# First loads on one queue in a fixed order, sums of x on VectorE, and a new order table in a seven-product interaction kernel

## The chip, the core and the metric

The kernel runs on one core of a Trainium2 chip. The metric is the device time of one execution in microseconds, as the median of several runs. A core has TensorE (PE; its weight loads are listed apart as PEld), VectorE (DVE), ScalarE (ACT), GpSimd (POOL) and SyncE (SP), and 16 DMA engines that all of them share. Plain transfers are issued here by SP, and a few by ACT; transfers that add what they bring to what lies in the destination are issued by POOL.

## What is computed

```python
out_lin = x @ lin_w.T + lin_b                                      # x: 1024 x 512
xv = jnp.einsum('bf,efm->bem', x, weight)                          # weight: 64 x 512 x 512
zp = jnp.einsum('bf,efm->bem', jnp.square(x), jnp.square(weight))
interaction = 0.5 * jnp.sum(jnp.square(xv) - zp, axis=1)
return out_lin + interaction                                       # 1024 x 512, float32
```

The sum over e of x² against weight² needs weight² only as its sum over e, so this is one matmul of the size of `x @ lin_w.T`. The large part is xv: x against 64 times 512 columns of weight, squared and summed over e.

## The kernel before

All matmuls are float32. Products of two matrices are made with seven products of quarters instead of eight (Strassen's scheme in Winograd's form), which trades matmuls for sums of operands and of results. It is used twice over, and the names follow from it.

**Outer level.** x (transposed, 512 features by 1024 rows) is cut into four quarters `x_in(h, q)`, h a half of the rows, q a half of the features. X1, X2 and X4 are copies of the quarters (0,0), (0,1), (1,1), made on ACT. X5 = x(1,1) - x(1,0), X6 = X5 - x(0,0) with a sign, X7 and X3 are combinations made on VectorE. The weight has four quarters too, w11, w12, w21, w22, and three sums: T1 (of the second and first quarter), T2 = a quarter + T1, then w12 + w22 and w21 + T2. These sums are not calculated by an engine: an adding transfer issued by POOL brings one operand into the other (`outer_sum`, L708 to L717, with `dma_add`, L480). Likewise, the results od are added to ob, and od to oc (`outer_out`, L719).

**Inner level.** Each of the seven pairs (X1 with w11, X6 with T2, X5 with T1, X2 with w21, X7 with w12, X4 with w21 + T2, X3 with w22, in this order, the constant `ORDER`) is multiplied again by seven products (`tree`, L749), or, for four of the seven in groups of 24 columns, by 20 products (`wide_tree`, L838). For this, each X gets further sums of its own four blocks: s1, s2, s4 and a new a21, four sums of 128x256 per X, 28 in all (L656 to L659). They go through `tt` (L438), which gives every sum that reads no PSUM to POOL unless it is told `only=DVE`. `widen` (L661) makes the further blocks for the trees of 20 later. The sums of weight blocks (tile `t`) are on POOL too.

**Stages.** The program begins with a memset and two warm-up matmuls of zeros (L554 to L559). Then `lin` (L623) makes x @ lin_w.T with the seven products of the outer level: 16 PE records each of 256 columns, at L543, in the order x1, x2, x4, x5, x6, x7, x3. It needs the quarters of lin_w, `lw(q, c)`, and sums of these (`lsum`), made on VectorE. Its four results go to DRAM (`lind`) and come back at the end. Then come 22 groups of columns of the weight, two of 16 columns and 20 of 24, each with the seven trees (L490). A group loads six pieces of weight on SP (`load`, L701). The squares of weights (ACT) are summed on VectorE (`w_squares`, L725), and so are the squares of xv (`finish`, L734). At the end the seven outer products of x² against the sums of weight² are made, on the same code as lin, and added to what lin left and to the accumulated sums (`accd`).

**PSUM.** Four pairs of banks, b1, b3, b2_0 and b2_1. A tree starts two products in b3 and two in b1, copies b1 to b2 on ACT, copies b3 to p5 and p53, and adds in the banks; the results leave to oa, ob, oc and od through VectorE. Trees of neighbouring pairs overlap on PE.

**What sets the order.** No order is written by hand. `Plan.add` (L171) takes each operation with its cost on an engine, and `Plan.order` (L196) goes through the program with these costs, giving each engine the most urgent operation that is ready. The urgency is the latest time at which it may start, less an entry of the table `AHEAD_OF` (in eighths of a microsecond, base 36). Every kind of operation in every part of the program has such an entry, so a new table can change the order on every engine. Each engine then runs its instructions strictly in the planned order, and each waits for its operands.

**The first loads.** x comes in eight transfers of 128x512 (0.262 MB) on SP; lw in four of the same size on ACT, through an argument `queue` of `dma` (L477) that only these use; then the bias. All are ordered by the planner.

Of the kernel before, what the change touches and what calls it, by code (L numbers as in the profile page):

```python
# [12 lines left out]
AF = mybir.ActivationFunctionType  # L13
# [28 lines left out]
i:-g j:4x k:t l:-8 m:-2k n:1x o:4i6 p:2c q:9 r:-1w s:n t:-11 u:-1 v:-o w:17 x:1n y:1z z:k 10:-23 11:g 12:-16  # L42
13:4 14:24 15:r 16:-5 17:z 18:j 19:-k 1a:13 1b:-18 1c:e 1d:-2z 1e:4 1f:21 1h:17 1i:-f 1j:-k 1k:-1 1l:1m 1m:-5
1n:-26 1o:-o 1p:q 1q:-b 1r:1p 1s:-22 1t:9 1u:-10 1v:-5 1w:8 1x:-9 1y:i 1z:1u 20:1e 21:-10 22:o 23:-n 24:-2x
25:2 26:-2t 27:-1z 28:2c 29:1b 2a:1z 2b:-b 2c:22 2d:-23 2e:1p 2f:4 2g:-2y 2h:-j 2i:1h 2j:o 2k:9 2l:k 2m:-c
2n:1i 2o:-1z 2p:-2 2q:47 2r:2n 2s:-6 2t:c 2u:-20 2v:10 2w:-2 2x:-m 2y:-10 2z:i 30:4p 31:5c 32:1j 33:9 34:2x
35:n 36:-6 37:-2c 38:d 39:1e 3a:-n 3b:r 3c:1t 3d:j 3e:m 3f:2k 3g:-2s 3h:1v 3i:31 3j:-12 3k:-m 3l:-2f 3m:7b
3n:2 3o:1co 3p:-i 3q:e 3r:-1h 3s:1nz 3t:-1l 3u:3 3v:118 3w:17 3x:-x 3y:-1t 3z:n 40:r 41:4 42:-v 43:18 44:2pm
45:1j 46:-l 47:-t 48:-1c 49:l3 4a:b 4b:2g 4c:e 4d:36 4e:y 4f:1v 4g:16 4h:-q 4i:b 4j:1 4l:-1r 4m:-3c 4n:n 4o:z
4p:-f 4q:-1d 4r:13 4s:5 4t:y 4u:2g 4v:4 4w:1i 4x:1c 4y:-20 4z:1z 50:l 51:-12 52:-20 53:27 54:-z 55:9 56:-2s  # L50
57:1o5 58:g 59:-1j 5a:-2r 5b:2k 5c:i 5d:21 5e:-12 5f:-1q 5g:1ju 5h:2d 5i:25 5j:p 5k:-1l 5l:-k 5m:-1y 5n:3b
5o:h 5p:-3r 5q:20 5r:-28 5s:-b 5t:2a 5u:29 5v:-n 5w:-2b 5x:w1 5y:3 5z:-1e 60:22 61:-1u 62:24i 63:-1u 64:-33
65:5m 66:-r 67:3q 68:-13 69:11 6a:22 6b:p 6c:s 6d:-y 6e:e 6f:25 6g:k 6h:-o 6i:-1n 6j:1c 6k:-u 6l:u 6m:e8
6n:-2f 6o:-1j 6p:z 6q:1m 6r:23 6s:-x 6t:h 6u:-15 6v:-29 6w:-y 6x:15 6y:-6j 6z:19 70:-n 71:-1n 72:-7 73:1u
74:-1n 75:-2c 76:-1e 77:3p 78:1q 79:7 7a:-2 7b:-u 7c:16 7d:-t 7e:-13 7f:-13 7g:-m 7h:u 7i:-1 7j:1c 7k:2b 7l:1p
7n:r 7o:-d 7p:b 7q:-w 7r:-3a 7s:u 7t:-20 7u:-v 7v:2c 7w:-32 7x:-8c 7y:1a 7z:-5 80:2i 81:-e 82:-2a 83:-2j
84:-29 85:-27 86:-j 87:d 88:-16 89:-2v 8a:-1g 8b:-c 8c:fk 8d:-c 8e:-g 8f:-2d 8g:-k 8h:i 8i:1i 8j:z 8k:-5
8l:-1a 8m:-dh 8n:-a 8o:-d1 8p:a 8q:-k 8r:-f 8s:s 8t:28 8u:q 8v:-19 8w:-1b 8x:3n 8y:-26 8z:fo 90:2s 91:-24 92:b
93:a2 94:-6 95:1h 96:1f 97:2q 98:-2u 99:-39 9a:-1j 9b:-m 9c:-2e 9d:28 9e:-s 9f:yw 9g:-l 9h:-16 9i:-w 9j:a
9k:ln 9l:-j 9m:1 9n:n 9o:1s 9p:-17 9q:r 9r:2p 9s:7 9t:-i 9u:m 9v:41 9w:3h 9x:-2c 9y:-s 9z:-17 a0:7 a1:-t a2:j  # L60
a3:-1x a4:1p a5:5 a6:-a a7:2k a8:-2g a9:14 aa:-u ab:-r ac:-14 ad:7 ae:-r af:-1a ag:-1w ah:-d ai:1vp aj:1a
ak:14 al:-1n am:-v an:w ao:-1b ap:1s aq:u ar:z as:11 at:-11 au:1q av:15 aw:j ax:-1b ay:-2i az:1d b0:-38 b1:-3t
b2:-k b3:n b4:-4 b5:-e b6:-j b7:-17 b8:le b9:-x ba:-1a bb:c0 bc:1 bd:he be:3m bf:-x bg:1u3 bh:a bi:38 bj:1sj
bk:-1j bl:c bm:-4q bn:-13 bo:-3h bp:1 bq:-4n br:-1j bs:1de bt:3w bu:1j bv:-8 bw:26 bx:17 by:d bz:-1c c0:-26
c1:3o c2:2c c3:1v c4:t c5:-2h c6:-4 c7:-2g c8:-h0 c9:y ca:3c cb:-u cc:-7i cd:-1 ce:-12 cf:-i cg:c ch:-2j
ci:-92 cj:-m ck:y cl:-1a cm:-m cn:7 co:10 cp:-19 cq:-i cr:-q cs:-15 ct:-1 cu:g cv:10 cw:19p cx:2g cy:-46 cz:2
d0:-1e d1:-1f d2:vf d3:s d4:-r d5:l9 d6:c8 d7:4r d8:-13 d9:-39 da:-t db:rq dc:-w dd:11 de:4o dg:d dh:-3 di:h
dj:-1b dk:2i dl:-b dm:-39 dn:3 do:1 dp:w dq:-1 dr:-r ds:4 dt:-6g du:-4 dv:20 dw:-5o dx:-3o dy:-1r dz:1t e0:3r
e1:-m e2:e e3:1d e4:-1b e5:b e6:-1j e7:-e9 e8:-6 e9:-cq ea:3c eb:1mv ec:-y ed:m ee:w ef:1x eg:1q eh:-1z ei:-w
ej:1l ek:-h el:2 em:f en:30 eo:b ep:1h eq:14 er:o es:6b et:-3 eu:-u ev:10x ew:1f ex:-x ey:-b ez:s f0:-2k f1:m  # L70
f2:-3r f3:e f4:1l f5:p f6:24 f7:-19 f8:9 f9:-4f fa:9ny fb:35 fc:-69 fd:d fe:-1a ff:-1k fg:g fh:z fi:-20 fj:cs
fk:-1i fl:-17f fm:1x fn:-7 fo:2w fp:h fq:jm fr:1s fs:n ft:mz fu:d fv:g fw:fq fx:p fy:-1y fz:-o g0:-h g1:-1x
g2:-4k g3:265 g4:15 g5:-m g6:-g g7:1t g8:-1m g9:-2b ga:-18 gb:2z gc:-9 gd:-2l ge:-1p gf:12 gg:8b gh:1k gi:2bs
# [1089 lines left out]
```

## Time and profile before

| | |
|---|---|
| median of three runs | 1412.26 us (1411.76 to 1416.25) |
| the profiled execution | 1414.87 us, of which span 1413.1 |
| granted TensorE clock, mean | 0.994 |
| busy share of the span | PE 98%, VectorE 83%, POOL 83%, ScalarE 58% |
| PE matmul records | 5500 (two for each float32 matmul) |
| chain that ended last | 91% PE, 4% DMA, 3% POOL |

The times of single steps below come from the one profiled execution. A row of the profile names source line, engine, operation, output tile and input tiles (with buffer numbers left out, so that w11, w12 and w21 all read `w`, T2 reads `T`, and X1 to X7 read `X`). Busy time of PE is no measure of PE at its peak, because matmuls overlap; where it counts, the distance from one matmul to the next is used.

### The profile page before, as it was taken

The page shows a single profiled execution, that of the slowest core. Times are in us where ns is not written, and L with a number is a line of the kernel's source. Part 1 is how long each engine was busy: PE and PEld are TensorE (multiplying, and loading weights), DVE is VectorE, ACT ScalarE, POOL GpSimd, SP SyncE. Part 2 cuts the span into 40 slices and gives each one's busy share as a digit, 9 for nine tenths or more (in the row PEclk, how much of TensorE's full clock was granted, in tenths as well). Part 3 has the DMA queues.
Part 4 walks back from the last instruction along what each step waited for, and adds up shares of the span by engine and source line. Part 5 has one row for each costly group of instructions (what it writes and reads, how often), then busy time and mean ns, then how long its engine had stood idle before and what let it go on. Part 6 is the DMA issues. An engine that isn't in the chain of part 4 may idle for free.

```text
span 1413.1 us, 17921 instructions
## 1 busy us (share of the span) xinstructions
PE 1388.7 (98%) x5500; PEld 1034.9 (73%) x5500; DVE 1179.7 (83%) x1769; ACT 825.7 (58%) x1345; POOL 1173.6 (83%) x1118
## 2 busy tenths in 40 slices
PE   7999999999999999999999999999999999999998
PEld 5878767677776767777776777777677777767666
DVE  5577788888988888888888888888888888898876
ACT  3355555757566565756656565666656565665752
POOL 5999978888788878878887887888788798888884
PEclk8999999999999999999999999999999999999999
DMA  8588595867859596775959577595957759594775
GB/s 248 150 191 195 111 254 126 221 164 178 202 122 243 122 232 154 184 195 127 242 115 247 144 179 199 134 236 116 254 136 183 194 145 228 117 257 117 162 171 131
DMA packets 94943, 251.85 MB, mean 178 GB/s; under 512 B 30464, under 2 KB 33536, under 8 KB 94848
## 3 DMA queue, kind: packets, MB, share of 16 engines
q0 software_dynamic: 27712, 136.23, 49.3%
q1 hardware_dynamic: 66560, 113.43, 23.6%
q10 hardware_dynamic: 576, 1.05, 0.2%
q8 instruction: 45, 0.74, 0.2%
q14 instruction: 50, 0.41, 0.1%
HBM read 127.04 MB, written 6.19 MB: 94 GB/s over the span
## 4 chain that ended last, share of the span: by engine, by line
PE 91%; DMA 4%; POOL 3%; issue 1%; DVE 1%; ACT 0%; SPq 0%; POOLq 0%; ACTq 0%
PE b L490 40%; PE b_r L490 24%; PE b_l L490 24%; POOL t L446 2%; PE b_l L543 2%; PE b_r L543 1%; DMA T<-T1b 1%; DMA oc<-od 1%; DMA T<-T1a 1%; DMA oa<-xT 1%; POOL ob L482 0%; DMA T1a<-weight 0%; DMA w22a<-weight 0%; POOL X L446 0%; DVE oa L446 0%
## 5 line engine op out<-in xcount | busy, mean ns | idle before, releaser
L490 PE MATMUL b<-t,X 128*128 128x384 f32 (+1 forms) x1184 | 401.9, 471 | 3.8 <-DVE ob L446 2.1
L446 POOL TENSOR_TENSOR t<-t,w 128x512 f32<-128x512 f32 (+1 forms) x300 | 293.9, 998 | 36.0 <-PE b L490 25.2
L490 PEld LDWEIGHTS b<-t,X 128*128 128x128 f32 x1184 | 219.2, 190 | 131.2 <-DVE ob L446 10.1
L490 PE MATMUL b_l<-t,X 128*128 128x256 f32 x960 | 243.4, 380 | 0.0
L490 PE MATMUL b_r<-t,X 128*128 128x256 f32 x800 | 214.8, 380 | 0.2 <-POOL t L446 0.2
L490 PEld LDWEIGHTS b_l<-t,X 128*128 128x128 f32 x960 | 180.7, 190 | 34.1 <-ACT b_l L456 2.5
L446 POOL TENSOR_TENSOR t<-w 128x768 f32<-128x768 f32 (+1 forms) x88 | 160.2, 1824 | 33.2 <-DMA w<-T 21.2
L490 PEld LDWEIGHTS b_r<-t,X 128*128 128x128 f32 x800 | 150.3, 190 | 46.0 <-issue 2.8
L463 ACT ACTIVATE oa<-oa 128x768 f32<-128x768 f32 (+1 forms) x176 | 142.7, 823 | 58.6 <-DVE oa L446 47.7
L473 DVE TENSOR_REDUCE acc<-oa 128x12 f32<-128x768 f32 (+1 forms) x176 | 159.2, 921 | 6.8 <-ACT oa L463 6.6
L473 DVE TENSOR_REDUCE w_sum<-wsq 128x12 f32<-128x768 f32 (+1 forms) x176 | 159.1, 919 | 1.4 <-ACT wsq L463 1.2
L490 PE MATMUL b_r<-w,X 128*128 128x256 f32 x600 | 149.7, 380 | 0.5 <-issue 0.5
L490 PEld LDWEIGHTS b_r<-w,X 128*128 128x128 f32 x600 | 112.8, 190 | 20.2 <-ACT b_r L455 1.9
L463 ACT ACTIVATE wsq<-w 128x768 f32<-128x768 f32 (+1 forms) x132 | 107.0, 819 | 32.6 <-DMA w<-weight 22.1
L490 PE MATMUL b_l<-w,X 128*128 128x256 f32 x480 | 117.5, 381 | 0.9 <-ACT b_l L456 0.9
L490 PE MATMUL b<-w,X 128*128 128x384 f32 (+1 forms) x336 | 110.2, 456 | 2.1 <-DMA w<-T 2.1
L456 ACT COPY b<-b 128x768 f32<-128x768 f32 (+1 forms) x74 | 55.4, 748 | 92.0 <-PE b L490 56.8
L490 PEld LDWEIGHTS b_l<-w,X 128*128 128x128 f32 x480 | 90.3, 190 | 17.1 <-ACT b_l L456 4.7
L463 ACT ACTIVATE ob<-ob 128x768 f32<-128x768 f32 (+1 forms) x88 | 72.0, 822 | 47.4 <-DVE ob L446 45.3
L490 PE MATMUL b<-T,X 128*128 128x384 f32 (+1 forms) x264 | 90.3, 477 | 2.2 <-DMA T<-T1a 1.4
L490 PEld LDWEIGHTS b<-w,X 128*128 128x128 f32 x336 | 63.5, 190 | 30.7 <-DMA w<-T 2.5
L473 DVE TENSOR_REDUCE acc<-oc 128x12 f32<-128x768 f32 (+1 forms) x88 | 79.8, 920 | 5.0 <-ACT oc L463 4.8
(179 smaller groups left out, 2620.1 us busy)
## 6 DMA issues: line engine op xcount, KB each, us to landing
w<-weight SPq DMA_DIRECT2D x120, 384.0 KB, 6.9
ob<-od POOLq DMA_DIRECT2D x40, 768.0 KB, 11.4
oc<-od POOLq DMA_DIRECT2D x40, 768.0 KB, 12.9
T<-weight SPq DMA_DIRECT2D x40, 384.0 KB, 5.8
w<-T POOLq DMA_DIRECT2D x20, 768.0 KB, 5.8
T1a<-weight SPq DMA_DIRECT2D x20, 384.0 KB, 3.3
T1a<-weight POOLq DMA_DIRECT2D x10, 768.0 KB, 8.4
w22a<-weight SPq DMA_DIRECT2D x20, 384.0 KB, 10.9
```

The lines of the kernel that those rows point to most:

```text
L446: return f(o.ap, a.ap, b.ap)
L456: return nc.scalar.copy(o.ap, i.ap)
L463: lambda _: nc.scalar.activation(o.ap, i.ap, AF.Square, scale=scale),
L473: nc.vector.tensor_reduce(o, x, axis=AX.X, op=ALU.add)
L490: nc.tensor.matmul(a.ap, b.ap, w.ap, start=start, stop=True, skip_group_check=True)
L543: nc.tensor.matmul(a.ap, b.ap, w(k).ap, start=first and k == 0 and j % 2 == 0, stop=True, skip_group_check=True)
```

## The change

1. **First loads.** All twelve loads of x and lw and then the bias go on SP, and in the order of the program text (`first_load` passes a `rank`, which replaces the urgency). The text now interleaves them: x(0,0) first block, lw(0,0), x(0,0) second block, x(0,1) first block, lw(1,0), x(0,1) second block, lw(0,1), lw(1,1), x(1,1), x(1,0), bias. The planner's costs for them are new.
2. **Sums of x blocks.** The four sums of each of X6, X5, X2, X7 and X4 (`PREP`) are given to VectorE; those of X1 and X3 stay on POOL.
3. **Three adding transfers.** T2 += T1 in groups 0 and 1 and w21 += T2 in group 0 (`DIRECT`) become sums of 128x1024 on VectorE. The same test in `outer_out` compares with the names of tiles and never holds.
4. **The table** `AHEAD_OF` is a new one, and two costs that the planner takes for the end (loads of lind, adds from accd) are larger.
5. A second way to make sums of weight squares (`SUMMED`) is added to the text, but its list is empty; of it only a small tile `unread` is there.

On the engines, VectorE has 23 instructions more, POOL 23 fewer (20 sums, three transfers), ACT four issues fewer and SP four more. The matmuls are the same 5500 records in another order.

```diff
+SUMMED = ()
+DIRECT = ((0, 2), (1, 2), (0, 4))
+PREP = (6, 5, 2, 7, 4)
 AHEAD_OF = """
-0:t6x 1:t29 2:2qu 3:2w 4:3gd7 5:2mat 6:-i 7:t4v 8:1kwd 9:1xp9 a:v6a b:xxr c:-4 d:3jg2 e:-r f:-j g:-r h:-2g
+0:t6e 1:t2s 2:2s5 3:3s 4:3geo 5:2mao 6:-1g 7:t51 8:1kv2 9:1xpj a:v57 b:xxu c:-17 d:54au e:-g f:-1e g:-o h:-4m
...
-            o.latest = latest - ahead[o.sign]
+            o.latest = latest - ahead[o.sign] if o.rank is None else o.rank - 1e6
...
-    def dma(o, i, reads, writes, moves=1.3, land=1.8, queue=nc.sync, issue=0.4):
-        plan.add({SP: issue}, lambda _: queue.dma_start(o, i), reads, writes, land=land, queue=moves)
+    def dma(o, i, reads, writes, moves=1.3, land=1.8, issue=0.4, rank=None):
+        plan.add({SP: issue}, lambda _: nc.sync.dma_start(o, i), reads, writes, land=land, queue=moves,
+                 rank=rank)
...
+    firsts = iter(range(100))
+
+    def first_load(o, i):
+        n = next(firsts)
+        dma(o.ap, i, (), o.atoms, 1.1 if n < 4 else 0.65, 2.2, 0.45, n)
+
     def lw_in(q, c):
-        o = lw(q, c)
-        dma(o.ap, lw_src[:, ts(q * 2 + c, KH * C)], (), o.atoms, 0.65, 2.2, nc.scalar, 0.25)
-
-    def x_load(h, q):
-        for k in range(KH):
-            o = x_in(h, q, k)
-            dma(o.ap, x_src[:, q * KH + k, ts(h, H)], (), o.atoms, 0.65, 2.2, issue=0.25)
-
+        first_load(lw(q, c), lw_src[:, ts(q * 2 + c, KH * C)])
+
+    def x_load(h, q, k):
+        first_load(x_in(h, q, k), x_src[:, q * KH + k, ts(h, H)])
+
+    x_load(0, 0, 0)
     lw_in(0, 0)
-    x_load(0, 0)
+    x_load(0, 0, 1)
+    x_load(0, 1, 0)
     lw_in(1, 0)
-    x_load(0, 1)
+    x_load(0, 1, 1)
     lw_in(0, 1)
     lw_in(1, 1)
-    x_load(1, 1)
-    x_load(1, 0)
-    dma(bias.ap, lin_b.partition_broadcast(P), (), bias.atoms, 1.3, 2.2)
+    for h, q in ((1, 1), (1, 0)):
+        for k in range(KH):
+            x_load(h, q, k)
+    first_load(bias, lin_b.partition_broadcast(P))
...
-            tt(o, a, b, sub)
+            tt(o, a, b, sub, DVE if i in PREP else None)
...
+        elif (g, which) in DIRECT:
+            tt(o, o, reg(i, 0, n), only=DVE)
         else:
             dma_add(o.ap, reg(i, 0, n).ap, n, reg(i, 0, n).atoms, o.atoms)
...
-        dma(four(r), lin_dram[:, c, ts(h, 4), :], (("lin", h, c),), r.atoms)
+        dma(four(r), lin_dram[:, c, ts(h, 4), :], (("lin", h, c),), r.atoms, 2.3)
...
-        dma_add(four(r, 0, cut), acc_dram[:, c, ts(h, 4), :cut], 4 * C,
+        dma_add(four(r, 0, cut), acc_dram[:, c, ts(h, 4), :cut], 5 * C,
```

More of the change, by code (lines that the diff above doesn't have):

```diff
@@ L45 @@
[L45 to L49, printed above, removed]
@@ L416 @@
     p53_ring = ring([make(f"p53_{k}", WIDE if thin else 2 * V) for k in range(P53S)])
-    wsq_ring = ring([make(f"wsq{k}", WIDE) for k in range(2)])
+    wsq_ring = ring([make(f"wsq{k}", WIDE) for k in range(2 if len(SUMMED) < 4 else 0)])
+    unread = make("unread", E)
     for name in ("b1", "b3", "b2_0", "b2_1"):
```

235 lines of the change are left out of this document (130 added, 105 removed).

## Prediction

> **What bounds the kernel now.** I read the page's first lines, then the busy time by stretches, then PE's waits, then the timeline of the first 45 us. The stretches (columns: stretch, length, busy us of each engine with its count, PEclk, DMA share, GB/s):
>
> ```profile
> 4.00:8.00 4.00, 1.01 (x2) 0.00 (x0) 0.29 (x1) 1.04 (x1) 1.55 (x2) 0.99 0.91 285
> 8.00:12.00 4.00, 0.00 (x0) 0.00 (x0) 0.00 (x0) 1.04 (x1) 0.00 (x0) 0.50 0.98 376
> ...
> 12.60:18.20 5.60, 5.58 (x13) 4.46 (x14) 5.14 (x6) 1.61 (x2) 4.52 (x5) 0.50 1.01 340
> ...
> 40.00:60.00 20.00, 20.00 (x92) 16.57 (x91) 6.59 (x11) 6.97 (x12) 19.09 (x27) 1.00 0.47 150
> 60.00:80.00 20.00, 19.96 (x90) 16.44 (x88) 14.50 (x23) 8.07 (x14) 19.66 (x26) 1.00 0.89 188
> 80.00:100.00 20.00, 16.57 (x74) 13.84 (x75) 14.74 (x25) 11.78 (x23) 18.00 (x22) 1.00 0.99 230
> 100.10:103.50 3.40, 3.40 (x10) 2.58 (x9) 2.29 (x5) 1.77 (x4) 2.82 (x3) 0.50 0.00 0
> ...
> 200.00:1300.00 1100.00, 1099.01 (x4330) 812.49 (x4329) 953.58 (x1436) 675.65 (x1100) 920.09 (x846) 1.00 0.73 178
> ```
>
> From 200 to 1300 us PE stands still for 1 us of 1100: there PE's own work is the bound, and the change leaves that as it is. What can be won lies in the first 200 us and the last 60. PE's waits name it (total, times, longest; the first five from the first 200 us, the last from the whole span):
>
> ```profile
> PE b_l L543 <- DMA oa<-xT: 7.6, 1, 7.6
> PE b L490 <- DVE ob L446: 2.1, 1, 2.1
> PE b L490 <- DMA T<-T1a: 1.4, 1, 1.4
> PE b L490 <- POOL t L446: 1.2, 1, 1.2
> PE b_l L490 <- ACT b_l L456: 0.9, 1, 0.9
> ...
> PE b L490 <- DMA w<-T: 2.1, 1, 2.1
> ```
>
> The largest is at the start. The timeline there (start, length, what; idle before and its releaser), and two rows of the chain that ended last, from lin and from where the trees begin:
>
> ```profile
> 0.74 0.87 SPq L478 DMA_DIRECT2D oa<-xT  x2
> 2.49 2.67 ACTq L478 DMA_DIRECT2D ob<-lin_wT  x2
> 2.60 6.31 SPq L478 DMA_DIRECT2D oa<-xT  x4
> 5.21 1.04 ACT L456 COPY X<-oa 128x1024 f32<-128x1024 f32 x1 [2.98 <-DMA oa<-xT]
> 12.13 1.23 DVE L446 TENSOR_TENSOR X<-ob,oa 128x1024 f32<-128x1024 f32 x1 [5.55 <-DMA oa<-xT]
> 12.62 3.78 PE L543 MATMUL b_l<-ob,oa 128*128 128x256 f32 x8 [7.61 <-DMA oa<-xT]
> ...
> 30.18 1.73 PE b_l L543 x8
> 40.77 22.21 PE b L490 x100
> ```
>
> The pair of x blocks that is issued first lands by 5.2, but it is X2's. PE begins with x(0,0) times lw(0,0), and that x comes last: X5, which needs x(1,0), may start at 12.13, PE, done with its warm-up at 5.0, only at 12.62. At full clock eight records take 1.73 us, so one of lin's seven products (16 records) 3.46. The first 5.6 us of lin ran at clock 0.50: half of it, 2.8 us, is lost.
>
> **The first loads (remove 10 us).** SP before, and SP now, at the program's start (oa and ob hold x, ob also lw):
>
> ```order
> L478 DMA oa_77<-xT 128x512 x2
> L478 DMA ob_78<-xT 128x512 x2
> L478 DMA oa_77<-xT 128x512 x4
> L478 DMA od_80<-lin_b 128x512
> L478 DMA w11_69<-weight 128x512 x2
> ```
>
> ```order
> L485 DMA oa_77<-xT 128x512
> L485 DMA ob_78<-lin_wT 128x512
> L485 DMA oa_77<-xT 128x512 x2
> L485 DMA ob_78<-lin_wT 128x512
> L485 DMA oa_77<-xT 128x512
> L485 DMA ob_78<-lin_wT 128x512 x2
> L485 DMA ob_78<-xT 128x512 x2
> L485 DMA oa_77<-xT 128x512 x2
> L485 DMA od_80<-lin_b 128x512
> L485 DMA w11_69<-weight 128x512 x2
> ```
>
> ACT's four issues went to SP, and what PE needs first comes first. The bytes are the same, 12 loads of 0.262 MB; 285 GB/s from 4 to 8 and 376 from 8 to 12 are 0.92 and 0.70 us a load. I take the first two as landed at 4.9 (X2's pair was there before 5.2, issued from the same place), the sixth at 8.3, the eighth at 9.8, the tenth at 11.1, the twelfth at 12.6, the bias at 14. The weights keep their place behind them.
>
> PE then starts at 4.9 instead of 12.62. x1 runs to 8.4 (0.1 lost on the third load), x2 to 11.9. x4 needs three VectorE sums over lw (0.7 each, the seventh and eighth load ahead of them) and a small one: 12.1. x5 needs the bias add (0.7, from 14) and X5 (1.23) behind it: 15.9, 0.4 after x4's end. Copies between products take 0.6. In all 24.2 of products and 1.5 of waits: lin ends at 30.6, where before the trees begin at 40.77. No stop is long, so I count full clock throughout. **Minus 10**: 7.7 from the start, the rest the clock.
>
> **VectorE sums for x and T2 (give back 1.5 us).** 20 sums of 128x256 (X6, X5, X2, X7, X4) leave POOL, three of 128x1024 replace transfers. The nearest rows:
>
> ```profile
> 13.60 1.75 DVE L587 SCALAR_TENSOR_TENSOR X<-X,oa 128x1024 f32<-128x1024 f32 x1
> ...
> 16.00 0.68 DVE L446 TENSOR_TENSOR w22b<-ob 128x512 f32<-128x512 f32 x1
> 18.08 1.26 POOL L446 TENSOR_TENSOR t<-w 128x512 f32<-128x512 f32 x1
> 21.49 1.46 DVE L446 TENSOR_TENSOR T1b<-ob,w22b 128x512 f32<-128x512 f32 x1
> 24.02 1.74 DVE L446 TENSOR_TENSOR X<-oa 128x1024 f32<-128x1024 f32 x1
> 25.68 2.28 DVE L587 SCALAR_TENSOR_TENSOR X<-oa,X 128x1024 f32<-128x1024 f32 x1
> 28.49 0.67 DVE L473 TENSOR_REDUCE w_sum<-wsq 128x8 f32<-128x512 f32 x1
> 29.08 0.68 DVE L446 TENSOR_TENSOR od<-b_r,od 128x512 f32<-128x512 f32 x1
> ...
> L446 POOL TENSOR_TENSOR X<-X 128x256 f32<-128x256 f32 x48 | 43.2, 949 | 18.8 <-ACT X L456 6.0 <-DVE X L446 5.5 <-PE b_r L543 4.6
> ```
>
> No row shows a 128x256 sum of SBUF alone on VectorE. Alone it lies under the 0.68 of twice its size, beside POOL under 1.46; I take 0.45, and 0.97 beside POOL (in the ratio of 1.46 to 0.68). The place that matters is the end of lin. VectorE before and now, over lin's last results (b1, b2 are banks; T1b, od, oc hold lin's sums):
>
> ```order
> L446 TENSOR_TENSOR oc_79<-T1b_75,b1_r 128x512
> L446 TENSOR_TENSOR od_80<-b1_r,od_80 128x512
> L446 TENSOR_TENSOR oc_79<-T1b_75,b2_0_l 128x512
> L446 TENSOR_TENSOR oc_79<-T1b_75,b2_0_r 128x512
> L446 TENSOR_TENSOR oa_77<-b2_0,p53_0_84 128x2x256
> ```
>
> ```order
> L453 TENSOR_TENSOR oc_79<-T1b_75,b1_r 128x512
> L453 TENSOR_TENSOR od_80<-b1_r,od_80 128x512
> L453 TENSOR_TENSOR X6_67<-X6_67 128x256
> L453 TENSOR_TENSOR oc_79<-T1b_75,b2_0_l 128x512
> L480 TENSOR_REDUCE w2_sum_91<-wsq1_87 128x8
> L453 TENSOR_TENSOR X6_67<-X6_67 128x256
> L453 TENSOR_TENSOR oc_79<-T1b_75,b2_0_r 128x512
> L453 TENSOR_TENSOR T2_76<-T2_76,T1a_74 128x1024
> L480 TENSOR_REDUCE w2_sum_91<-wsq0_86 128x8
> L601 SCALAR_TENSOR_TENSOR X2_63<-X2_63 128x128
> L453 TENSOR_TENSOR oa_77<-b2_0,p53_0_84 128x2x256
> ```
>
> T2 += T1, once a transfer beside lin, now stands behind every result of lin; behind it wait POOL's difference of T2 (1.26) and PE's tree 6. From the first sum over lw (9.0) to T2's end VectorE has 32 instructions: 18 that read PSUM or reduce, which follow each other by 0.6 (28.49, 29.08), 10.8; four sums of 512, five of 256, three of 1024 and two scaled ones of 1024. Alone that is 10.8 + 2.7 + 2.3 + 3.7 + 3.5 = 23.0. Until 16 us POOL reads little; beside POOL are at most the three later 256s, X7, T2 and the scaled two: 10.8 + 2.7 + 0.9 + 1.2 + 2.9 + 3.5 + 4.6 = 26.6. With 0.5 lost on the bias T2 is there between 32.5 (not before lin's last result, 30.8 + 0.7 + 1.2) and 36.1, and tree 6 may begin between 34.0 and 37.4, where PE arrives ten matmuls of 0.43 after 30.6, at 34.9. Of 0 to 2.5 I take **plus 1.5**, nearer the end beside POOL, which is busy then.
>
> The Trainium skill ("SBUF — State Buffer", "Who interferes with whom") says that a VectorE instruction with two SBUF inputs and a GpSimd one that reads SBUF shut each other out for a whole instruction, a rule against this part: by it the upper end holds and the sum is 1 us worse. The rows of 0.68 and 1.46, of one size, agree in direction.
>
> The other moved sums, ten to twelve us of them, lie in 40 to 80, where VectorE is busy 21 of 40 us, which hides them; without that slack each would cost its 0.45 to 1.2. POOL, busy 39 of 40 us there, is rid of 20 x 0.95 and of three DMA issues.
>
> **Groups 0 to 1 (remove 4 us).** The chain of waits at 82 to 99, the timeline's two rows on the second add, issues by kind with their median to landing, and the queue's share:
>
> ```profile
> 82.67 13.97 DMA oc<-od
> 96.66 0.64 ACT oc L463
> ...
> 97.93 0.69 DVE ob L446
> 83.42 1.69 POOL L482 DMA_DIRECT2D oc<-od  x1
> ...
> 99.93 0.63 ACT L463 ACTIVATE oc<-oc 128x512 f32<-128x512 f32 x1 [0.60 <-DMA oc<-od]
> ob<-od POOLq DMA_DIRECT2D x4, 512.0 KB, 8.6
> q0 software_dynamic: 27712, 136.23, 49.3%
> ```
>
> PE waited 2.1 for a VectorE result behind a reduction of oc's square, and this for the adding transfer. The queue was full (DMA 0.99 after 0.47 from 40 to 60), because POOL came late. POOL before and now, around the add of T1b, group 1's first:
>
> ```order
> L446 TENSOR_TENSOR t_81<-w22a_72,t_81 128x256
> L446 TENSOR_TENSOR X4_65<-X4_65 128x256 x2
> L482 DMA T1b_75<-weight 128x1024
> L446 TENSOR_TENSOR t_81<-w11_69 128x2x256
> L446 TENSOR_TENSOR X4_65<-X4_65 128x256
> ```
>
> ```order
> L453 TENSOR_TENSOR t_81<-T2_76,t_81 128x256 x2
> L453 TENSOR_TENSOR t_81<-w12_70,t_81 128x256
> L453 TENSOR_TENSOR X3_64<-X3_64 128x256 x2
> L490 DMA T1b_75<-weight 128x1024
> L453 TENSOR_TENSOR X3_64<-X3_64 128x256
> L453 TENSOR_TENSOR X1_62<-X1_62 128x128 x2
> ```
>
> It stood behind group 0's last sums and group 1's first followed; now it stands between group 0's trees 6 and 7 and leaves the crowded stretch, as do the adds of w21 and T2. 49.3% of 1413 us for 136.23 MB is 5.1 us a MB, 2.7 a transfer of 0.52 MB: three make 8 of the 38 us of DMA work between 60 and 100. The stalls there cost 2.1 + 1.2 and, by the clock of 0.50, half of 3.4: 5.0. Now oc's first add comes after matmul 76 of group 0 (32.1 + 76 x 0.43 = 65, two results and the issue: 67.5), and ACT needs it at matmul 110, 79. At 8.6, like ob, it is in time; I leave 1: **minus 4.** The waits on T<-T1a, on ACT, and on w<-T at the end have their chains unchanged, and I count nothing for them: minus 4 if the new table clears them, plus 2 if two POOL sums more (0.95 each) stand ahead of w21's last add.
>
> **Sum:** 10 - 1.5 + 4 = 12.5. The profiled execution took 1414.87 (span 1413.1), so 1402.4; the median of the runs is 1412.26, so **1399.8**. A difference within 0.3%, 4.2 us, could not be told from none.
>
> **Rivals.**
> - *The start is partly paid back at the seam of groups 0 and 1* (0.18). For: ACT now has oc's first square ahead of the copy that frees tree 1's bank. If oc's two adds take 14.0 and 16.5 as before, the first is there at 81.5, 2.5 late, the second (70.7 + 16.5, needed at 82 + 2.5) 2.7 late, and the clock halves once, 1.7: 6.9 instead of 5.0. Then 10 - 1.5 - 1.9, 1405.7. Against: the lighter queue. The Trainium skill ("TensorE: Matmul & The Clock Gate", "What's actually happening") has the clock throttled after an idle window of about 3.4 us; by that the 1.7 falls away, 1404.0. The trace halved after a stop of 2.1, so I keep it.
> - *One queue keeps the pace of its first two loads*, 1.2 us each (0.08): the twelfth lands at 16.8, X5 is done at 18, x5 2 us later and the clock may halve: 1403.
> - *Slower by the new table* (0.06): where tree 3 of a group meets tree 1 of the next, PE takes two matmuls of tree 3 ahead of four of tree 1, once in two groups, so 1.7 us sooner. If POOL's operand came just in time before, ten such places cost 17: 1417. It decides from 1.7 a place. Against: 1 us idle of 1100, POOL busy 920 of them.
> - *More than forecast* (0.12): the waits on T<-T1a, ACT and w<-T go too, T2 is in time: 1394.
>
> **Numbers.** The forecast has 0.56, 1396 to 1404. The range reaches from 1391.5 (all late waits gone) to 1408.5 (most of the seam rival). Faster: 0.56 + 0.12 + 0.07 + half of the seam rival, 0.84; same, its other half, 0.09; slower 0.07.
>
> **What would show it.** Lin's first matmul at 5 us with clock near 1 up to 18; lin's end at 30 to 31; a wait of 0 to 3 us at tree 6, on POOL t or DVE T; T1b's add issued near 40; oc's adds landing in under 11 us; 200 to 1300 as before. It is wrong if PE waits over 4 us between 30 and 45, over 4 near 80, or over 5 in 200 to 1300.

## The result, and the profile after

The changed kernel takes 1400.44 us (median of 4 runs, 1398.8 to 1402.83) against 1413.49 us for the kernel before beside it (4 runs, 1411.76 to 1416.25): a ratio of 0.9907, 95% interval 0.9883 to 0.9931. The forecast was 1399.8. The profiled execution took 1398.8 us (span 1396.9, granted clock 1.0 in the mean) against 1414.87 (span 1413.1). This pair lies 16 us apart, the medians 13; some 3 us of what follows are the difference between single executions.

First the stretches of the changed kernel (columns as before: stretch, length, busy us of PE, its weight loads, VectorE, ACT and POOL with counts, clock, DMA share, GB/s):

```profile
4.00:8.00 4.00, 4.00 (x11) 2.46 (x10) 0.29 (x1) 1.04 (x1) 0.55 (x1) 1.00 0.96 311
8.00:12.00 4.00, 4.00 (x20) 3.52 (x19) 2.51 (x3) 2.68 (x4) 3.84 (x5) 1.00 1.05 367
12.60:18.20 5.60, 5.60 (x27) 4.65 (x26) 5.54 (x7) 0.00 (x0) 3.08 (x3) 1.00 1.05 393
40.00:60.00 20.00, 17.85 (x80) 14.65 (x80) 18.76 (x26) 5.02 (x9) 14.69 (x21) 1.00 0.34 75
60.00:80.00 20.00, 19.96 (x90) 16.49 (x90) 17.98 (x29) 9.46 (x17) 16.89 (x20) 1.00 0.94 205
80.00:100.00 20.00, 18.66 (x87) 16.12 (x87) 16.84 (x28) 13.23 (x25) 16.61 (x22) 1.00 0.64 156
200.00:1300.00 1100.00, 1099.95 (x4333) 814.63 (x4332) 955.82 (x1440) 674.48 (x1098) 928.27 (x855) 1.00 0.74 179
```

PE works from the start at full clock, where before it stood still from 8 to 12 us and then had 0.50. From 40 to 60 us it now stands still for 2.15 us, and VectorE is the busiest of the others there: 18.76 of 20 us, where it had 6.59 before. In 40 to 80 together it went from 21 to 37 of 40 us. From 80 to 100 us the DMA share is 0.64 instead of 0.99. PE's waits (total, times, longest):

```profile
PE b_r L557 <- ACT b_r L463: 2.7, 1, 2.7
PE b L498 <- DVE X L453: 2.2, 1, 2.2
PE b_l L573 <- DVE t L568: 1.6, 1, 1.6
PE b L498 <- ACT b L463: 1.3, 1, 1.3
PE b_l L498 <- ACT b_l L463: 1.3, 1, 1.3
PE b L498 <- DMA T<-T1a: 0.9, 1, 0.9
```

The waits of 7.6 on the first loads and of 2.1 on w<-T at the end are gone, the one of 2.1 on VectorE's `ob` is down to 0.5; the first two rows are new. The timeline shows where they come from (start, length, what; idle before and its releaser):

```profile
5.16 2.80 PE L557 MATMUL b_l<-ob,oa 128*128 128x256 f32 x8
...
26.39 1.23 ACT L470 ACTIVATE wsq<-w 128x512 f32<-128x512 f32 x2 [3.12 <-DVE w_sum L480]
27.52 0.58 ACT L463 COPY b_r<-b_r 128x512 f32<-128x512 f32 x1
...
28.15 1.99 PE L557 MATMUL b_r<-w22b,X 128*128 128x256 f32 x8 [2.70 <-ACT b_r L463]
...
33.44 1.03 PE L498 MATMUL b<-t,X 128*128 128x256 f32 x4
...
34.24 1.22 DVE L453 TENSOR_TENSOR T<-T,T1a 128x1024 f32<-128x1024 f32 x1
...
41.56 3.32 POOL L453 TENSOR_TENSOR X<-X 128x256 f32<-128x256 f32 x6
...
45.56 1.13 PE L498 MATMUL b<-T,X 128*128 128x256 f32 x4 [2.15 <-DVE X L453]
...
86.75 0.63 ACT L470 ACTIVATE oc<-oc 128x512 f32<-128x512 f32 x1 [1.66 <-DMA oc<-od]
87.28 0.58 ACT L463 COPY b<-b 128x512 f32<-128x512 f32 x1
88.01 0.67 PE L498 MATMUL b<-t,X 128*128 128x256 f32 x2 [1.33 <-ACT b L463]
```

Lin's first matmul is at 5.16 (forecast 4.9). Lin ends at 33.4, not at 30.6: its product x7 needs a bank that ACT copies free, this copy stood behind two squares of w11, and these waited 3.12 us for a buffer that VectorE's reductions give back. T2's sum on VectorE came at 34.24 and ended at 35.46, and PE did not wait for it. It waited later in tree 6, for X6's last sum. Ahead of that one on VectorE stood a sum of X5, of which the tile's rows say (durations min, median, max in ns; first and last start):

```profile
L453 DVE TENSOR_TENSOR X<-X x1: 3843/3843/3843, 41.3 to 41.3; 128x256 f32<-128x256 f32 x1
```

3.84 us, while POOL ran six sums of X blocks in a row from 41.56. By the trace, the 20 such sums of X on VectorE take 0.41 us at the least, 0.68 in the median, and the next longest takes 1.49.

To see every loss and not only the named waits, I took from the trace, for each matmul, the distance to the start of the next one, less the distance that such matmuls have when nothing holds them (0.216 us for 256 columns, 0.323 for 384; for the four warm-up records of 512, which no trace shows unheld, 0.429 as an estimate from these, the same in all kernels). The sums over stretches, in us, of all kernels; E1 to E12 are the experiments below:

| stretch (us) | before | after | E1 | E2 | E3 | E4 | E5 | E6 | E7 | E8 | E9 | E10 | E11 | E12 |
|---|---|---|---|---|---|---|---|---|---|---|---|---|---|---|
| 0 to 20 | 12.1 | 3.0 | 11.9 | 2.7 | 3.0 | 10.2 | 12.1 | 10.1 | 3.0 | 3.0 | 2.9 | 3.2 | 2.7 | 2.8 |
| 20 to 60 | 1.6 | 6.1 | 4.6 | 6.9 | 7.9 | 11.0 | 7.5 | 3.0 | 6.1 | 7.1 | 7.2 | 3.9 | 4.6 | 5.4 |
| 60 to 100 | 4.9 | 2.4 | 2.7 | 6.0 | 17.2 | 4.4 | 11.0 | 4.0 | 2.4 | 2.5 | 5.2 | 2.4 | 2.3 | 13.6 |
| 100 to 200 | 6.5 | 4.4 | 5.6 | 4.4 | 6.9 | 5.1 | 16.2 | 5.5 | 4.3 | 4.8 | 6.3 | 4.9 | 5.3 | 5.6 |
| 200 to 1300 | 10.9 | 6.8 | 7.3 | 8.7 | 8.0 | 11.2 | 8.3 | 10.0 | 8.3 | 8.7 | 9.4 | 10.3 | 7.8 | 8.8 |
| 1300 to the end | 4.1 | 1.4 | 1.3 | 1.3 | 1.3 | 4.7 | 1.7 | 4.0 | 1.3 | 1.3 | 6.8 | 1.3 | 1.3 | 1.4 |
| sum | 40.2 | 24.0 | 33.4 | 30.0 | 44.3 | 46.5 | 56.8 | 36.5 | 25.3 | 27.5 | 37.7 | 26.0 | 24.0 | 37.5 |

Before less after is 16.2, which is the difference of the spans. Of it, 9.1 come from the first 20 us, 4.5 are given back up to 60, and 2.5, 2.1, 4.1 and 2.7 come from the four later stretches. Of the 2.1 from 100 to 200 us, 1.4 belong to the seam of groups 0 and 1: before, the clock was at half from 100.1 to 103.5.

### The profile page after: what moved, and what is told of

It reads as the page before. It is cut to its first block, busy times and chain, and to the rows that moved or that the text cites. A ratio compares the mean times of both kernels' runs of the same rounds, so it can differ in the third digit from the quotient of the medians.

```text
span 1396.9 us, 17915 instructions
## 1 busy us (share of the span) xinstructions
PE 1381.5 (99%) x5500; PEld 1034.9 (74%) x5500; DVE 1195.9 (86%) x1792; ACT 824.4 (59%) x1345; POOL 1159.7 (83%) x1095
## 4 chain that ended last, share of the span: by engine, by line
PE 91%; POOL 4%; DMA 3%; DVE 2%; issue 1%; SPq 0%; ACT 0%; POOLq 0%; DVEq 0%; ACTq 0%
PE b L498 41%; PE b_l L498 24%; PE b_r L498 24%; POOL t L453 2%; PE b_r L557 1%; PE b_l L557 1%; DMA oc<-od 1%; DMA T<-T1a 1%; DVE X L453 1%; POOL X L453 0%; DMA w<-T 0%; DMA ob<-od 0%; DMA ob<-lin_wT 0%; POOL ob L490 0%; DVE X L601 0%
## 5 line engine op out<-in xcount | busy, mean ns | idle before, releaser
L498 PE MATMUL b_l<-t,X 128*128 128x256 f32 x960 | 247.0, 380 | 0.0
L453 POOL TENSOR_TENSOR t<-w 128x768 f32<-128x768 f32 (+1 forms) x88 | 163.4, 1860 | 35.0 <-DMA w<-T 18.5
L463 ACT COPY b_l<-b_r 128x512 f32<-128x512 f32 x80 | 46.1, 577 | 85.8 <-PE b_r L498 53.1
## 6 DMA issues: line engine op xcount, KB each, us to landing
oc<-od POOLq DMA_DIRECT2D x40, 768.0 KB, 12.5
```

What stands on the lines that cost most here:

```text
L453: return f(o.ap, a.ap, b.ap)
L463: return nc.scalar.copy(o.ap, i.ap)
L498: nc.tensor.matmul(a.ap, b.ap, w.ap, start=start, stop=True, skip_group_check=True)
```

## The experiments

In all of them but E9, every engine keeps the order of the kernel that the experiment is made from: the planner works with unchanged costs, and only what is issued at a place is replaced, or a few instructions are moved by hand. Medians are of 4 to 10 runs, ratios are to the kernel before beside them.

### E1 and E6: the first loads, taken back and alone

E1 is the changed kernel with the old arrangement of loads, E6 the kernel before with the new one.

```diff
 # E1
+PUT, ON_ACT = (3, 5, 9, 8, 11, 10, 7, 1, 0, 2, 4, 12, 6), (1, 4, 6, 7)
...
+        pairs.append((o.ap, i))
+        def emit(_):
+            return (nc.scalar if PUT[n] in ON_ACT else nc.sync).dma_start(*pairs[PUT[n]])
 # E6
+PUT = (1, 0, 2, 4, 3, 5, 6, 7, 8, 9, 10, 11, 12)
...
+        if len(first) < len(PUT):
+            first.append((o, i))
+            emit = lambda _: nc.sync.dma_start(*first[next(taken)])
```

> The changed kernel with every engine's order kept, only its first twelve loads issued as before (x on SP with X2's blocks first, lw on ACT). Theory A (the first loads carry about half of the gain of 13 us, the new order most of the rest): lin's first matmul at 12 to 13 us instead of 5.2, a stretch at clock 0.5 there, the program 7 to 10 us longer than the changed one, so 1407 to 1410. Rival B (the loads carry nearly all): 12 or more longer, 1412 or above. Rival C (VectorE is the late engine from 15 us on, so that early loads bring little): 2 to 5 longer, 1402 to 1405, with lin's end at most 3 us later than 33.4.

> The kernel before with every engine's order kept, only its twelve first loads on SP in the new order. Theory A (first loads worth about half): lin's first matmul at 5 instead of 12.6, the clock near 1 from 7 us on; lin's end 7 to 9 us earlier, and the program 6 to 8 shorter than before, 1405 to 1407, where tree 6 or the adding transfers behind it may take 1 or 2 back. Rival B (loads carry nearly all): 11 to 13 shorter, 1400 to 1402. Rival C (what follows lin is late anyway, by POOL and the weights): 1 to 4 shorter, 1409 to 1412.

E1: 1408.87 us, ratio 0.9965 (0.9945 to 0.9985), 8.4 longer than the changed kernel; lin's first matmul at 12.50. This is theory A's number. E6: 1411.99, ratio 0.9997 (0.9986 to 1.0009): nothing, which is the upper end of rival C's range, but not its reason. The timeline of E6:

```profile
9.04 1.04 ACT L457 COPY X<-oa 128x1024 f32<-128x1024 f32 x1 [6.82 <-DMA oa<-xT]
11.72 1.04 ACT L457 COPY X<-ob 128x1024 f32<-128x1024 f32 x1 [1.63 <-DMA ob<-xT]
12.67 1.04 ACT L457 COPY X<-oa 128x1024 f32<-128x1024 f32 x1
13.61 0.58 ACT L457 COPY b_l<-b_l 128x512 f32<-128x512 f32 x1
...
5.16 2.14 PE L551 MATMUL b_l<-ob,oa 128*128 128x256 f32 x8
...
14.24 3.78 PE L551 MATMUL b_l<-ob,oa 128*128 128x256 f32 x8 [5.22 <-ACT b_l L457]
```

PE starts at 5.16, as in the changed kernel. But in the old order ACT copies three quarters of x to X2, X4 and X1 first, and the copy of lin's first bank stands behind them. PE stops for 5.22, the clock falls to half from 12.5 to 19.3, and the trees begin at 39.87 instead of 40.77. So the loads are worth 8 to 9 us in the changed kernel's order and nothing in the old one. That ACT's order is what matters is read from this timeline; no run changed it alone.

### E2: the sums of x back on POOL

```diff
-            tt(o, a, b, sub, DVE if i in PREP else None)
+            tt(o, a, b, sub, DVE if i in PREP else None, on=POOL)
```

> The changed kernel with every position in the order kept, only the twenty sums of X6, X5, X2, X7 and X4 run on POOL. Theory A (these sums make VectorE late in the start, 2.7 us at lin's product x7 through ACT and 2.2 us in tree 6): both waits fall under 1, but POOL has 20 x 0.95 us more and is late for tree 6 and for group 1: 3 to 8 us longer in all, 1403 to 1408. Rival C (POOL has slack in the start, and VectorE's lateness is pure loss): 2 to 5 us shorter, 1395 to 1398.

1404.25 us, ratio 0.994 (0.9919 to 0.9961): 3.8 longer, theory A. The wait through ACT fell from 2.7 to 1.6 only, and a new wait of 3.2 on a POOL sum of X came at 76 us, after which the clock halved for 3.4 us. VectorE pays for these sums up to 60 us (6.1 against 1.6 before), but POOL would pay more: 6.9 up to 60, and 6.0 instead of 2.4 from 60 to 100.

### E3 and E12: the adding transfers back, all three and one

```diff
-            tt(o, o, reg(i, 0, n), only=DVE)
+            i = reg(i, 0, n)
+            plan.add({DVE: 0.08 + 1.06 * n / 1024},
+                     lambda _: nc.gpsimd.dma_start(o.ap, i.ap, accum_op=ALU.add),
+                     o.atoms + i.atoms, o.atoms, both=True)
```

E12 does this for T2 of group 1 alone.

> The changed kernel with every position in the order kept, only the three sums (T2 += T1 twice, w21 += T2) run as adding transfers. Theory A (they lie on the path at tree 6 and in the full queue of groups 0 to 1): T2 of group 0 is issued at about 34.3 and lands 6 to 8 us later instead of after 1.2, so tree 6 waits 4 to 6 us, and oc's adds take 12 to 16 us: 6 to 10 longer, 1406 to 1410. Rival B (transfers were hidden by the order): within 2 us of the changed kernel, 1399 to 1403.

> The changed kernel with every position in the order kept, and only group 1's T2 += T1 run as an adding transfer again; T2 of group 0 and w21 stay sums. With all three back the program was 19 us longer, and there this transfer took 13.5 us from issue to landing and POOL waited 11.8 for it. Theory K (it alone costs most, since POOL's next instruction needs it and PE stops behind POOL and ACT): issue near 78, landing 10 to 14 us later, a stop of PE of 7 to 11 us between 85 and 105 and the clock halved once or twice behind it, 8 to 14 longer than the changed kernel, 1408 to 1414. Rival L (the three crowd one another, and alone it lands in 8 us or less): 1402 to 1406.

E3: 1419.71 us, ratio 1.005 (1.0035 to 1.0065), 19 longer than the changed kernel; more than either theory expected. E12: 1415.27, ratio 1.0018 (1.0006 to 1.0029), 15 longer: theory K, a little above its range. POOL and then PE in E12:

```profile
75.44 1.58 POOL L733 DMA_DIRECT2D T<-T1b  x1
88.81 1.26 POOL L453 TENSOR_TENSOR t<-T 128x512 f32<-128x512 f32 x1 [11.78 <-DMA T<-T1b]
...
93.27 1.22 PE L498 MATMUL b<-T,X 128*128 128x256 f32 x2 [10.12 <-ACT oa L463]
```

The transfer stands behind the adds of ob and oc and lands 13.3 us after its issue. POOL waits for it, a sum of results stands behind that wait on POOL, ACT's square of this sum waits 11.8 us, and the copy that frees PE's bank stands behind the square. One transfer stops three engines, and the clock is at half for 10.2 us from 88.1 on. In the kernel before the same transfer took 10.3 us (77.19 to 87.46, by the trace) and nobody waited for it, because POOL came to the sum that reads it only then:

```profile
77.19 1.33 POOL L482 DMA_DIRECT2D T<-T1b  x1
...
88.02 2.20 POOL L446 TENSOR_TENSOR t<-T 128x512 f32<-128x512 f32 x1
```

It is the order that uncovers it: before, eleven POOL instructions stand between this issue and the sum that reads T2, in the new order none, since there T2 is a VectorE sum of 1.22 us (at 76.44 in the changed kernel). So 15 us are the price of a transfer in an order made for a sum. What it would cost after the earlier start in an order planned for it, no run shows. The issues by kind show what is left of the queue (KB each, median us to landing):

```profile
q0 software_dynamic: 27280, 134.66, 49.4%
...
ob<-od POOLq DMA_DIRECT2D x4, 512.0 KB, 5.7
oc<-od POOLq DMA_DIRECT2D x4, 512.0 KB, 10.5
```

### E4 and E5: operations and order exchanged

E4 is the kernel before with all three edits of operations put in place; E5 is the changed kernel with all three undone. The edits are those above and their mirror images.

> The kernel before with the old order and all three edits of operations put in place: loads on SP in the new order, the twenty X sums and the three adding sums on VectorE where POOL had them. The first four runs showed: new loads in the old order are worth nothing, old loads in the new order cost 8, the three adding transfers in the new order cost 19. Theory D (operations pay only in an order made for them): 1409 to 1416, no more than 4 us from before, with a wait of 4 us or more at lin on ACT's copy behind X4's copy, and losses of 1.6 to 1.9 us in each 200 us from 500 on. Rival E (the edits pay by themselves, mostly the adding sums, by the queue they relieve): 1403 to 1407.

> The changed kernel's order with all three edits of operations undone in place: loads as before, the X sums on POOL, the three sums as adding transfers. Theory D: worse than each undone alone, 1420 to 1430, with waits over 10 us in groups 0 to 1, yet from 500 to 1300 us losses of 1.0 to 1.3 us in each 200 us and no wait on the transfer w<-T at the end. Rival F (the new order is better in itself): 1400 to 1410.

E4: 1421.38 us, ratio 1.0058 (1.0045 to 1.0072), 9 longer than before, beyond theory D's upper end. PE waits 5.3 for ACT as in E6, and then 7.5 for VectorE's sums over lw, of which one takes 7.44 us, the others 0.68 at the least. The timeline of E4 shows what POOL does meanwhile:

```profile
19.37 7.44 DVE L449 TENSOR_TENSOR w22b<-ob,w22b 128x512 f32<-128x512 f32 x1
...
19.47 1.03 POOL L449 TENSOR_TENSOR t<-w,t 128x256 f32<-128x256 f32 x1
20.16 1.69 POOL L449 TENSOR_TENSOR X<-X 128x256 f32<-128x256 f32 x2
21.52 1.54 POOL L449 TENSOR_TENSOR t<-w 128x512 f32<-128x512 f32 x1
22.74 0.73 POOL L449 TENSOR_TENSOR X<-X 128x128 f32<-128x128 f32 x1
23.15 1.66 POOL L449 TENSOR_TENSOR t<-w,t 128x256 f32<-128x256 f32 x2
24.51 1.51 POOL L449 TENSOR_TENSOR t<-T1a 128x512 f32<-128x512 f32 x1
25.71 1.14 POOL L492 DMA_DIRECT2D w<-w22a  x1
```

Eight POOL sums follow each other, and VectorE's ends when POOL turns to issuing a transfer. E5: 1434.9, ratio 1.0152 (1.0137 to 1.0167), beyond theory D's range too. New operations in the old order cost 9, the new order with old operations 22; both together gain 13. Two rows of the table of losses go with the order or table, whatever the operations. From 1300 us to the end all kernels with the old order or table lose 4.0 to 6.8, all with the new one 1.3 to 1.7. From 200 to 1300 us the former lose 9.4 to 11.2 (mean 10.4 of four), the latter 6.8 to 10.3 (mean 8.3 of ten); these two ranges overlap, and each value is one execution.

### E9: the changed kernel planned with the old table

The text of the changed kernel with the numbers of `AHEAD_OF` from before, so that the planner orders the new operations by its own costs.

> The changed kernel planned with the old table, so that the planner orders the new operations by their own costs and dependences, but with the old corrections. Theory D (the edits need the new table): 1408 to 1420, no faster than before by more than 4 us, the wait on the transfer w<-T at the end back in some place, losses of 1.6 or more in each 200 us from 500 on. Rival J (the planner finds a fitting order by itself, the table gives only 3 to 5 us): 1402 to 1406.

1411.95 us, ratio 0.9994 (0.9981 to 1.0008): theory D. The edits without the new table gain nothing that can be measured. PE's waits:

```profile
PE b L496 <- DVE ob L451: 3.3, 2, 1.9
PE b_r L555 <- ACT b_r L461: 2.9, 1, 2.9
PE b L496 <- ACT p L461: 2.0, 1, 2.0
PE b L496 <- DMA w<-T: 2.0, 1, 2.0
...
PE b L496 <- DMA T<-T1a: 1.6, 1, 1.6
```

The start is as good as in the changed kernel (2.9 lost up to 20 us), so here the planner found an order for the start by itself. The rest is spent later: 7.2 us from 20 to 60, 5.2 and 6.3 up to 200, and 6.8 from 1300 on, where the wait on w<-T is back.

### E7, E8, E10, E11: VectorE in the start

These move instructions of the changed kernel (a pair is: which, behind which).

```diff
+    steps = plan.order()
+    for n, behind in MOVED:
+        x = next(s for s in steps if s[0].n == n)
+        steps.remove(x)
+        steps.insert(1 + next(k for k, s in enumerate(steps) if s[0].n == behind), x)
 # E7: ACT's squares of w11 behind the copy of lin's bank
+MOVED = ((120, 54), (118, 120), (121, 118))
 # E8: five POOL sums of X blocks behind POOL's next sum of results
+MOVED = ((513, 154), (511, 513), (650, 511), (649, 650), (646, 649))
 # E10: E8's, and VectorE's reductions of group 0 behind T2's sum, X6's last sum ahead of X5's
+MOVED = ((117, 109), (115, 117), (120, 128), (118, 120), (291, 118), (78, 132), ...
 # E11: E10's, and one reduction of group 2 behind the sum that frees a bank
+MOVED = (..., (813, 579))
```

> The changed kernel, with one ACT copy of lin's bank b1 put ahead of the two squares of w11 that it stood behind. Theory A1 (that copy alone held product x7): the wait of 2.7 us falls to under 0.5, lin ends at 30.5 to 31 instead of 33.4, and the program is 2 to 3 us shorter, 1397.5 to 1398.5. Rival A2 (VectorE is late with lin's results and T2 anyway): lin ends earlier, but a wait of 1.5 to 2.7 appears at tree 6 or between lin and tree 1, and the program is within 1 us of the changed kernel.

> The changed kernel, with five sums of X blocks on POOL put behind POOL's next sum of results, so that they no longer run in a row beside VectorE's sum of X5 (3.84 us there, 0.41 alone). Theory G (a run of POOL sums shuts a VectorE sum of two SBUF tiles out for as long as it lasts): the VectorE sum takes under 1.5 us, the wait of 2.2 us in tree 6 falls to under 0.5, and the program is 1.5 to 2.5 shorter, 1398 to 1399. Rival H (the 3.84 us are a wait on something else that the row hides): the sum still takes over 3 us, and the wait stays.

> The changed kernel with VectorE's load up to tree 6 lightened by order alone: the reductions of weight squares of group 0 and the squares that need their buffers stand behind T2's sum, X6's last sum stands ahead of X5's, and the five POOL sums of the run before stand later, as there. Theory A2 (VectorE is the late engine from 15 to 46 us: freeing the copy alone only moved its wait of 2.7 us to later ones): lin ends at 30.5 to 31, T2's sum begins at 31.5 to 32.5 instead of 34.2, no wait over 1 us stays between 20 and 50, the losses from 20 to 60 us fall from 6.1 to under 2.5, and the program is 3 to 5 us shorter than the changed one, 1395.5 to 1397.5. Rival I (another limit stands right behind: POOL's differences of T2, the weights, or the pushed-back squares on ACT): waits of 2 us or more remain there, and the program is within 1.5 us of the changed one.

> The version with the light start, and one more change of order: in group 2 a reduction of a weight square (0.95 us on VectorE) stands behind the sum that frees the bank for which ACT's copy, and PE behind it for 1.3 us, waited at 146 to 148 us. Theory A2 (small stops each cost their length once): this wait falls to under 0.5, the span is 0.8 to 1.2 us shorter than with the light start alone, about 1398, and against the kernel before the ratio is 0.988 to 0.991. Rival I: the wait moves to the next bank, and nothing is gained.

E7: 1398.33 us, ratio 0.9901 (0.9885 to 0.9918), not distinguishable from the changed kernel. The wait through ACT is gone, and the timeline of PE shows two others in its place:

```profile
30.42 1.03 PE L499 MATMUL b<-t,X 128*128 128x256 f32 x4
...
35.46 1.10 PE L499 MATMUL b<-t,X 128*128 128x256 f32 x4 [1.47 <-ACT b L464]
...
45.51 0.70 PE L499 MATMUL b<-T,X 128*128 128x256 f32 x2 [2.68 <-DVE X L454]
```

Lin ends 3.0 us earlier, and tree 6's wait ends at 45.5 as before: losses from 20 to 60 us are 6.1 in both. VectorE is what is late (A2), and ACT's copy was only where PE met it. E8: 1400.64, ratio 0.9916 (0.9902 to 0.9929). VectorE's two sums of X5 at the place in question, with one POOL sum beside the second instead of a row of six:

```profile
L454 DVE TENSOR_TENSOR X<-X x2: 899/1224/1549, 43.7 to 44.6; 128x256 f32<-128x256 f32 x2
```

The longest is 1.55 instead of 3.84, and the wait in tree 6 is gone, which agrees with theory G. It does not prove it. In E12 both engines have the order of the changed kernel here, the same row of six included, and yet the same sum (the second of these three) took 1.66, and PE's wait on X was 0.2:

```profile
40.65 3.19 DVE L453 TENSOR_TENSOR X<-X 128x256 f32<-128x256 f32 x3
41.81 3.80 POOL L453 TENSOR_TENSOR X<-X 128x256 f32<-128x256 f32 x6
```

The median of E8 is no shorter than the changed kernel's. In the profiled execution, the longest of its four, the wait through ACT was 3.0 us and the clock was at half from 27.6 to 34.4; the others have no trace. E10: 1399.28, ratio 0.9909 (0.9894 to 0.9924). Lin ends at 30.7, T2's sum begins at 31.90, no wait over 1 us is left from 20 to 50 us, and 3.9 are lost from 20 to 60 instead of 6.1; of theory A2's 3 to 5 us the start shows 2, the median 1, which its interval does not tell from none. E11: 1399.74, ratio 0.9901 (0.9884 to 0.9918): the wait at 146 to 148 stayed at 1.3 (rival I), because the sum that frees the bank now waited 0.79 us for PE's own result; nothing is gained. No version is shown to be faster than the changed kernel.

## Why the prediction was right, and where its steps were not

**The number.** 1399.8 against 1400.44, inside the range. The sum was 10 - 1.5 + 4 = 12.5 and the medians differ by 13, but the terms did not come out one by one: in the profiled pair the three together give 9.1 - 4.5 + 3.9 = 8.5 of its 16.2, and the rest comes from stretches that were counted at nothing. That the total fits is in part luck.

**The first loads (-10).** Measured -9.1 in the first 20 us, and +8.4 when they are taken back (E1). The size holds; the cause was told too narrowly. I read SP's order and the loads' landings, and did not look at what stands on ACT between the loads and lin's first copy. In the old order the loads give nothing (E6).

**VectorE's sums (+1.5).** The step that failed: measured +4.5 between 20 and 60 us. The sum of instructions up to T2 was right (its end was forecast between 32.5 and 36.1, and was 35.46), and T2 was not what PE waited for. VectorE's lateness reached PE by two ways that I had not followed: through the ring of two buffers for squares, by which ACT and its copy for x7 wait for VectorE's reductions (2.7), and through X6's last sum (2.2). E7 shows that the first way is only the nearer exit of the same lateness. The second hangs on a price: I took 0.97 for a sum of 128x256 beside POOL, and one took 3.84 beside a row of POOL sums. E4 has a second case, 7.44 us. With the row moved away it took 1.55 (E8), but in E12 1.66 with the row in place, so that the row alone does not explain it; the cause stays open. The rows behind my price were misread, too: the sum of 0.68 was not alone, a POOL sum ran beside it from 16.01 (1.25 us, by the trace). And the slack that was to hide the other moved sums, VectorE at 21 of 40 us from 40 to 80, was used up: 37 of 40.

The Trainium skill ("SBUF — State Buffer", "Who interferes with whom") has the two shut each other out for a whole instruction; the prediction set it against the rows and found a sum worse by 1 us by it. The trace agrees that the one can shut the other out, but not on the length: in the changed kernel the VectorE sum began ahead of six POOL sums by its row and ended behind the sixth.

**Groups 0 to 1 (-4).** Measured -2.5 from 60 to 100 us and -1.4 from 100 to 104, where the halved clock of the kernel before lies: the forecast size, nearly. The adds of oc landed in 10.4 and 11.2 us instead of 14.0 and 16.5; the 1 us left open became 1.33, by the path of the seam rival (ACT's square of oc ahead of the copy that tree 1 waits for). What the sums gave beside the queue's relief is not parted from the order: E12 shows only that in the new order T2 of group 1 as a transfer costs 15 us. I had looked at its share of the queue, and not at its 10 to 13 us to landing and at what stands between its issue and its reader.

**What was counted at nothing.** The wait on w<-T at the end (2.1) went. It goes with the order: 2.0 to 2.1 in the four kernels with the old order or table, at most 0.4 in the ten others. I had called its chain unchanged, though the order around it is the table's. The wait on T<-T1a fell from 1.4 to 0.9, the one on ACT's b_l rose from 0.9 to 1.3. From 200 to 1300 us, forecast as before, the pair shows -4.1 and the mean over kernels -2.1. In the pair, 2.7 at the end, 4.1 before it and 0.6 of 104 to 200 us are 7.4 us that the forecast did not have (5.4 with the mean over kernels); they covered the 4.0 by which its own terms fell short of 12.5.

**The table as such** was in the prediction only as a risk of +4.6. E9 shows that with the old one the edits gain nothing, and E4 and E5 that neither the new operations in the old order nor the new order with the old operations gain. What stays open is which of its entries matter after 100 us, and whether another table would do as well; neither was tried.

**The rivals.** The seam's path was there, at 1.33 us. One slow queue was not: by the trace the loads landed at 3.44, 5.02, 6.24, 7.40, 8.09 and then 0.66 us apart, the twelfth at 12.69. Of the signs, oc's second add landed in 11.2 us and not under 11, the wait at tree 6 was on X6 and not on T2, and 200 to 1300 did not stay as before.

## What to carry to other kernels

For each transfer on a crowded queue, list its time to landing and what the engine does between the issue and the instruction that reads it, and not only its share of the queue: one of 10 to 13 us held nobody up with eleven instructions between, and cost 15 us with none. An order made for one operation is not the order for another. Price an edit together with the order around it: for each wait that is to go, read what stands on every engine between its releaser and PE. And where two engines share a burden, follow the buffers between them, since a late engine shows up at whoever waits for its buffers.

## What was not expected of the hardware

- A VectorE sum of two SBUF tiles of 128x256 took 0.41 us alone, 1.55 beside one POOL sum (E8), 3.84 beside six in a row (the changed kernel; E1 the same, E7 3.95), but 1.66 beside the same six in E12; one of 128x512 took 7.44 beside eight (E4). In the changed kernel and E4 its row begins ahead of the first POOL sum, by 0.23 and 0.10 us, and yet it ended behind the last of them, by 0.3 and 0.8. In these cases, and in a shorter one in E6 (3.14, 128x512), POOL was still issuing an adding transfer when the row began, but so it was in E12. In the kernel before, where no issue stands there, VectorE had its turns between the sums of a POOL row (three sums of 512, 512 and 1024 columns from 21.49 to 25.76: 1.46, 1.21 and 1.74). What decides is open.
- The clock's fall to half after a stop of PE is not told by the stop's length: it fell after stops of 2.1 (before), 2.9 (E9), 3.0 (E8) and 3.2 us (E3), and did not after 2.7 (the changed kernel, E7) and 2.9 (E12). It then lasted 3.4, 6.8 or 10.2 us. These and the stretches at full clock between two falls are multiples of 3.41 us, so each trace can be cut into windows of 3.41 us, counted from a change of its clock. Up to 1380 us the fourteen traces then show 19 falls, all at the end of a window in which PE stood still for 1.91 us or more; at full clock it stayed in all windows with 1.90 or less, and in one with 1.95 (E6). The stop of 2.1 lies in one window for 1.99; E12's 2.9 is cut into 1.1 and 1.7, the changed kernel's 2.7 into 1.9 and 0.8. So what a stop costs depends on where it lies in these windows, which nobody chose, and the changed kernel's first one came close to a fall.
- The Trainium skill ("TensorE: Matmul & The Clock Gate", "What's actually happening") has windows of 3413 ns that run on by themselves, and a fall after at least one idle window. The lengths agree with the first; the falls with 1.91 to 2.2 us of standstill in a window do not agree with a whole idle one.
- An adding transfer of 0.52 MB from SBUF to SBUF landed 4.6 us after its issue in the kernel before (T2 of group 0, 26.83 to 31.39, by the trace) and 13.3 us after it in E12, where two adds of oc and one of w12 stood ahead of it.
